# Seven half-size products for the last product of a graph layer, with PSUM copies and one buffer less, in a fused two-layer graph network on one Trainium2 core

## The chip, the core and the metric

The kernel runs on one core of a Trainium2 chip. The core has a matrix engine (PE, with its weight loads shown apart as PEld), a vector engine (DVE), a scalar engine (ACT), a general engine (POOL, not used here beyond the set-up) and a synchronising engine (SP) whose queue issues all DMA transfers. Each engine works through its own list of instructions in order, and waits at semaphores for the others. Data lies in HBM outside the core, in SBUF (128 partitions) for operands, and in PSUM for what PE writes. The metric is the device time of one execution in microseconds; the time of a version is the median of its runs.

## The reference

32 graphs ("batches") of 512 nodes with 512 features go through two layers, all in fp32. Layer 0 is attention with 8 heads of 64 whose weights are multiplied by the adjacency, an output product, a residual and a layer norm. Layer 1 is a graph attention with one logit per pair of nodes.

```python
# layer 0
q = x @ Wq.T + bq ; k = x @ Wk.T + bk ; v = x @ Wv.T + bv      # 8 heads of 64
logits = q k^T / sqrt(64) + log(clip(adj, 1e-8))
out = softmax(logits) v @ Wo.T + bo
x = layer_norm(x + out) * gamma + beta
# layer 1
feat_proj = feats @ fc_w.T + fc_b
q = feat_proj @ q_w.T + q_b ; k = feat_proj @ k_w.T + k_b       # one number per node
masked = q + k^T + (1 - adj) * -1e9 ; leaky ReLU, slope 0.01
out = softmax(masked) @ feat_proj + feats
```

## The kernel before

**Tiling.** A 512x512 matrix is held as four chunks of 128 partitions. N and D are 512, P is 128, H is 256 (half a row), KH is 2 (half the chunks). Layer 1 is computed as z = e^T-weighted sum of the normalised rows n (`z`, matmul group pz), and then zT times fc (`out_units`, group pg), so the projection by fc comes after the weighted sum. Each row of the result is scaled by 1/r and added to yb, the residual, and stored (L457, L460).

**Seven products.** Several 512x512 products are done as seven products of half-size blocks with sums of blocks ahead and behind (the scheme of Strassen in Winograd's form): q and k together (`seven_qk`, L587, banks called f), v (`seven_v`) and Wo (`seven_wo`), these two through `seven` (L199, groups pv and pw). Their PSUM banks have names a, b, c (and d). "First" in a call of `mul` tells whether the bank is started afresh or added to. Product 6 of Wo reads data that a subtraction on DVE has turned first (L718).

**Order.** The order on PE, DVE, ACT and SP is written out by hand (`manual_schedule`), so what a function calls first comes first in the engine's list. The main loop runs over batches b and, in each, over four slots p, one for each pair of heads (`slot`). A slot does the scores of its pair (`score`, tile sc, in the two double banks of the pool ps_s), exponentials on ACT (L772, into tiles `at`), the multiplication by adjacency on DVE (`factors`, L780), the sums for the denominator on DVE (`sums`, L790 and L793), the value product of the pair before (`values`, po), and q and k of the pair after (`seven_qk`, which takes both banks of ps_s in turn). Later stages of earlier batches are laid in between:

- slot 0: the transposed weights eT of batch b-2 (`eT`, four DVE transposes of the blocks eP), then z of b-2, then yb of b-2 (`rest_of_layer1`);
- slot 1: Wo of b-1, the statistics of the norm, and the mask of e (L396); x again into n, and adj into e of b-1, are loaded ahead of the slot (`load_again`);
- slot 2: norm rows of b-1 on ACT, xT of b+1 (four DVE transposes), the last product of layer 1 of b-2 (`out_units`), the dots with uk and uq of b-1 (`dots`, L370), the spreading of k by a trip through DRAM;
- slot 3: block differences for the next batch (`differences`, L568 to L571), v of b+1, q and k of its first pair, and the softmax of b-1 (`softmax`: `logits` L409 and L410, `weights` L420 and L421, then 16 DMAs that write e in blocks into eP).

In the last batch, slot 3 is `last_slot`, which ends with the whole of layer 1 for batches 30 and 31.

**Buffers.** The tag L1 has two buffers of 8 KB a partition, for e, eT and zT. The tag x of the pool io has one, for x, the work tile w, and eP. `at` has six buffers, `as` two, and the pool ps_m three banks.

Of the kernel before, what the change touches and what calls it, by code (L numbers as in the profile page):

```python
# [19 lines left out]
P = 128  # L20
# [5 lines left out]
BL = 32  # L26
# [4 lines left out]
def kernel(  # L31
# [48 lines left out]

    nc = tc.nc
# [8 lines left out]
    assert 2 * DK == P and N == 512 and D == 512 and B >= 2  # L90
# [46 lines left out]
    def spread_blocks(dst, src):  # L137


        for i in range(P // BL):  # L140
            for j in range(P // BL):
                nc.sync.dma_start(
                    out=dst[j * BL : (j + 1) * BL, i, :].rearrange("r (m f) -> r m f", f=BL),
                    in_=src[i * BL : (i + 1) * BL, :, :].rearrange(
                        "r c (t q f) -> q r (c t) f", q=P // BL, f=BL)[j],
                )
# [10 lines left out]
    def load_constants():  # L157
# [10 lines left out]
        for name in ("v_s", "wo_s"):  # L168
            K[name] = const.tile([P, 3, KH, H], FP, name=name)
# [35 lines left out]
    def fold_units(psum, scratch):  # L205
# [57 lines left out]
        def spread():  # L263
# [8 lines left out]
            ps = psum.tile([P, D], FP, tag="m", name="ps_parts")  # L272
# [163 lines left out]
    def z_units(s, psum, name):  # L436

        def unit(d):
            pz = psum.tile([P, N], FP, tag="m", name=f"pz_{name}_{d}")
            product(pz, lambda i: s["n"][:, i, ts(d, P)], lambda i: s["eT"][:, i, :])  # L440
            nc.scalar.copy(s["zT"][:, d, :], pz)  # L441
        return [lambda d=d: unit(d) for d in range(DC)]
# [24 lines left out]
    def fast(ctx):  # L467
# [31 lines left out]
        def load_again(b):  # L499
            s = S[b]  # L500
            if b == B - 1:
                s["n"] = act.tile([P, NC, D], FP, tag="xT", name=f"n_{b}")
            elif b > 0:
                s["n"] = act.tile([P, NC, D], FP, tag="n", name=f"n_{b}")
            if b > 0:
                load_b(s["n"], x[b])
            if b < B - 1:
                s["e"] = act.tile([P, NC, N], FP, tag="L1", name=f"e_{b}", bufs=2)
                load_b(s["e"], adj[b])

        def load_last_e():

            S[B - 1]["e"] = cT
            load_b(cT, adj[B - 1])
# [59 lines left out]
        def seven_qk(b, p):  # L574
# [18 lines left out]
            def one(name):  # L593
                if name == "b":
                    mul(2, ps["b"], True)
                    add.append(lambda: nc.vector.tensor_add(q[:, :H], ps["b"], q[:, :H]))  # L596
                elif name == "a":
                    mul(1, ps["a"], True)
                    nc.scalar.activation(q[:, :H], ps["a"], AF.Identity, bias=bq)  # L599
                elif name == "c":  # L600
                    mul(5, ps["c"], True)
                    nc.scalar.activation(k[:, H:], ps["c"], AF.Identity, bias=bk)
                elif name == "d":
                    mul(4, ps["d"], True)
                    nc.scalar.activation(k[:, :H], ps["d"], AF.Identity, bias=bk, scale=-1.0)
                elif name == "a6":
                    mul(6, ps["a"], False)
                    nc.scalar.activation(q[:, H:], ps["a"], AF.Identity, bias=bq)
                elif name == "c3":
                    mul(3, ps["c"], False)  # L610
                    add.append(lambda: nc.vector.tensor_add(q[:, H:], ps["c"], q[:, H:]))  # L611
                elif name == "a7":
                    mul(7, ps["a"], False)
                    add.append(lambda: nc.vector.tensor_add(k[:, H:], ps["a"], k[:, H:]))
                    add.append(lambda: nc.vector.tensor_add(k[:, :H], ps["a"], k[:, :H]))

            add = []
            own = p % 2 == 1

            def unit(names):  # L620
                if not ps:
                    f = [
                        ps_s.tile([P, 2, N], FP, tag="s", name=f"f_{b}_{p}_{i}") for i in range(2)
                    ]
                    for i, name in enumerate("acbd"):
                        ps[name] = f[i % 2][:, i // 2, :H]
                    if own:
                        ps["b"] = ps_m.tile([P, H], FP, tag="m", name=f"pq_{b}_{p}")
                add.clear()
                for name in names:  # L630
                    one(name)
                for a in add:
                    a()
# [3 lines left out]
            names = (("b", "a", "c"), ("a6", "d"), ("a7", "c3"))  # L637
            if not own:
                names = (("a", "c", "b", "d"), ("a6", "c3"), ("a7",))
            return [lambda n=n: unit(n) for n in names]  # L640

        def seven_v(b):
# [13 lines left out]
            def unit0():  # L656
# [3 lines left out]
                nc.scalar.copy(c11, ps["a"])  # L660
                mul(2, ps["b"], True)
                nc.vector.tensor_add(c11, ps["b"], c11)

            def unit1():
                mul(5, ps["c"], True)
                nc.scalar.copy(c22, ps["c"])
                mul(6, ps["a"], False)
                nc.scalar.copy(c12, ps["a"])

            def unit2():  # L670
                mul(4, ps["b"], True)
                nc.scalar.activation(c21, ps["b"], AF.Copy, scale=-1.0)
                mul(3, ps["c"], False)
# [8 lines left out]
        def seven_wo(b, banks, apart=False):  # L682
# [3 lines left out]

            s = S[b]
            n, oT = s["n"], s["oT"]
            put = b > 0
            n11, n12, n21, n22 = (  # L690
                n[:, m : m + KH, ts(h, H)] for m in (0, KH) for h in range(2)
            )
            wo, W = K["wo"], K["wo_s"]
            right = {1: wo[:, :KH, :H], 2: wo[:, KH:, :H], 3: wo[:, KH:, H:], 4: W[:, 2],
                     5: W[:, 0], 6: W[:, 1], 7: wo[:, :KH, H:]}
            ps = {}

            def data(i, c):
                return {1: oT[c][:, :H], 2: oT[KH + c][:, :H], 3: oT[KH + c][:, :H],
                        4: oT[KH + c][:, H:], 5: oT[c][:, H:], 6: oT[c][:, :H],  # L700
                        7: s["s3"][:, c, :]}[i]

            def mul(i, to, first):
                seven(data, right, i, to, first)

            def seed():
                for name, bank in zip("bac", banks()):
                    ps[name] = bank
                for name, h in (("a", 0), ("c", 1)):
                    bo = K["bo"][:, ts(h, H)].unsqueeze(1).to_broadcast([P, KH, H])  # L710
                    if put:
                        nc.scalar.copy(ps[name], bo)

            def unit0():
                mul(1, ps["a"], not put)
                mul(2, ps["b"], True)
                for c in range(KH):
                    nc.vector.tensor_sub(oT[c][:, :H], oT[c][:, H:], oT[c][:, :H])  # L718
                nc.vector.tensor_add(n11, ps["a"], n11)
                for c in range(KH):  # L720
                    nc.vector.tensor_sub(oT[KH + c][:, :H], oT[KH + c][:, :H], oT[c][:, :H])
                nc.vector.tensor_add(n11, ps["b"], n11)

            def unit1():
                mul(5, ps["c"], not put)
                mul(6, ps["a"], False)
                nc.vector.tensor_add(n22, ps["c"], n22)
                nc.vector.tensor_add(n12, ps["a"], n12)

            def unit2():  # L730
                mul(3, ps["c"], False)
                mul(7, ps["a"], False)
                nc.vector.tensor_add(n12, ps["c"], n12)
                nc.vector.tensor_add(n22, ps["a"], n22)

            def unit3():
                if apart:
                    mul(4, ps["b"], True)
                    nc.vector.tensor_add(n21, ps["a"], n21)
                    nc.vector.tensor_add(n21, ps["b"], n21)  # L740
                else:
                    mul(4, ps["a"], False)
                    nc.vector.tensor_add(n21, ps["a"], n21)
            return [seed, unit0, unit1, unit2, unit3]
# [6 lines left out]
        def other_banks(b):  # L751

            def tiles():
                return [t.rearrange("p (n f) -> p n f", n=KH) for t in (
                    ps_m.tile([P, N], FP, tag="m", name=f"pw_{b}_b"),
                    ps_o.tile([P, N], FP, tag="po", name=f"pw_{b}_a"),
                    ps_s.tile([P, 2, N], FP, tag="s", name=f"pw_{b}_c")[:, 0, :],
                )]
# [117 lines left out]
        def divide_here(b, p):  # L876
# [20 lines left out]
            def refine():  # L897
                junk = S[b - 1]["w"][:, 0, :]
# [9 lines left out]
        def z(b):  # L908
            s = S[b]
            s["zT"] = act.tile([P, DC, N], FP, tag="L1", name=f"zT_{b}", bufs=2)  # L910
            return z_units(s, ps_m, b)

        def eT(b):
            s = S[b]
            s["eT"] = act.tile([P, NC, N], FP, tag="L1", name=f"eT_{b}", bufs=2)
            if b >= B - 2:
                return transpose_units(s["e"], s["eT"], ps_m, nc.scalar.copy, f"e_{b}")

            eP = s["eP"].rearrange("p q (c t f) -> p t c q f", c=NC, f=BL)
            return [lambda t=t: nc.vector.transpose(  # L920
# [439 lines left out]
```

## Time and profile before

| what | value |
|---|---|
| median of 3 runs | 3525.23 us (3522.59 to 3525.47) |
| profiled execution | 3527.14 us, its span 3525.4 us |
| mean granted TensorE clock | 0.998 |
| DMA | 250.66 MB in the span, mean 71 GB/s |
| chain that ended last | PE 96%, DVE 2% |
| one batch in the middle (b=15) | 1505.76 to 1614.22 us |
| q, k, v, Wo: matmuls of 128x256 | mean 379 to 405 ns of one |
| scores, values, pz, pg: matmuls of 128x512 (or 64x512) | mean 592 to 617 ns of one |

How to read it: the page gives busy time, the mean duration of one instruction, and the idle time ahead of a group with what ended it. A group of matmuls has overlapping members, so its mean duration is longer than the distance from one start to the next. Every fp32 matmul of the program appears as two records. In a timeline, each line is a run of like instructions: start, length, engine, line, operation, output and inputs, how many, and in brackets how long the engine sat idle and for what. "DVE 2%" in the chain is the share of the span in which the last chain of work ran through DVE.

### The profile page before, as it was taken

What the parts mean: (1) busy time and instruction counts of PE and PEld (TensorE: products, weight loads), DVE (VectorE), ACT (ScalarE), POOL (GpSimd) and SP (SyncE); (2) the same over time, 40 slices, a digit from 0 to 9 for tenths busy, and PEclk for the clock granted to TensorE, in tenths of its full rate; (3) what the DMA queues carried; (4) which work ended last, traced back from release to release, by engine and by line L of the source; (5) the groups of instructions that cost most, each with busy time, mean ns of one, the idle gap of its engine ahead of it and who ended that gap; (6) DMA issues with size and microseconds to landing.
All of it is one profiled execution on the core that took longest, in us unless ns stands there. A gap on an engine that the chain in (4) does not pass through costs nothing.

```text
span 3525.4 us, 38493 instructions
## 1 busy us (share of the span) xinstructions
PE 3503.8 (99%) x13834; PEld 2041.8 (58%) x13834; DVE 2739.6 (78%) x4690; ACT 1305.6 (37%) x2120; POOL 0.9 (0%) x9
## 2 busy tenths in 40 slices
PE   9999999999999999999999999999999999999999
PEld 3555665655556656555566565555665655556654
DVE  5788778788787787777877878878778777787786
ACT  3334333433334343333433343333434333343332
POOL 0000000000000000000000000000000000000000
PEclk9999999999999999999999999999999999999999
DMA  4244233443233442334423344333344233442321
GB/s 114 49 75 88 51 70 70 73 87 58 71 73 62 87 75 58 75 61 81 88 52 70 70 73 88 58 71 73 62 87 77 56 76 61 81 88 53 69 64 52
DMA packets 880461, 250.66 MB, mean 71 GB/s; under 512 B 807180, under 2 KB 807436, under 8 KB 880264
## 3 DMA queue, kind: packets, MB, share of 16 engines
q1 hardware_dynamic: 880264, 248.15, 35.6%
q8 instruction: 110, 1.80, 0.2%
q14 instruction: 87, 0.71, 0.1%
HBM read 181.93 MB, written 34.65 MB: 61 GB/s over the span
## 4 chain that ended last, share of the span: by engine, by line
PE 96%; DVE 2%; issue 0%; DMA 0%; ACT 0%; SPq 0%; DVEq 0%; ACTq 0%
PE f L587 19%; PE sc L767 14%; PE po L805 13%; PE pg L304 12%; PE pz L304 12%; PE pw_a L199 6%; PE pv_a L199 5%; PE pw_c L199 3%; PE pv_b L199 3%; PE pv_c L199 3%; PE pq L587 2%; PE ps L822 2%; PE pw_b L199 2%; PE pk L304 0%; PE pv L304 0%; DVE at L780 0%
## 5 line engine op out<-in xcount | busy, mean ns | idle before, releaser
L772 ACT ACTIVATE at<-sc 128x1024 f32<-128x1024 f32 x512 | 496.5, 1021 | 788.3 <-PE sc L767 786.5
L780 DVE SCALAR_TENSOR_TENSOR at<-cT,at 128x1024 f32<-128x1024 f32 x512 | 601.7, 1217 | 175.2 <-ACT at L772 175.0
L767 PE MATMUL sc<-qT,kT 64*128 64x512 f32 x2048 | 510.6, 617 | 0.5 <-DVE qT L611 0.5
L805 PE MATMUL po<-at,v 128*64 128x512 f32 x2048 | 469.0, 600 | 0.0
L304 PE MATMUL pz<-eT,n 128*128 128x512 f32 x1024 | 445.4, 592 | 0.0
L304 PE MATMUL pg<-fc,zT 128*128 128x512 f32 (+1 forms) x1032 | 445.3, 589 | 0.0
L767 PEld LDWEIGHTS sc<-qT,kT 64*128 64x128 f32 x2048 | 176.7, 186 | 295.8 <-issue 268.2
L304 PEld LDWEIGHTS pg<-fc,zT 128*128 128x128 f32 x1032 | 195.8, 190 | 231.8 <-issue 215.2
L304 PEld LDWEIGHTS pz<-eT,n 128*128 128x128 f32 x1024 | 194.2, 190 | 231.0 <-issue 221.1
L805 PEld LDWEIGHTS po<-at,v 128*64 128x64 f32 x2048 | 135.7, 137 | 318.2 <-issue 315.3
L793 DVE TENSOR_TENSOR as<-as,at 128x1024 f32<-128x1024 f32 x254 | 308.3, 1214 | 5.5
L587 PE MATMUL f<-T,qk_s 128*128 128x256 f32 x992 | 244.8, 379 | 6.4 <-DVE qT L596 4.8
L441 ACT COPY zT<-pz 128x512 f32<-128x512 f32 x128 | 74.8, 585 | 425.4 <-PE pz L304 425.4
L587 PEld LDWEIGHTS f<-T,qk_s 128*128 128x128 f32 x992 | 185.0, 190 | 36.3 <-DVE qT L596 5.6
L587 PE MATMUL f<-xT,wq 128*128 128x256 f32 x744 | 191.0, 379 | 0.0
L813 ACT COPY oT<-po 128x512 f32<-128x512 f32 x128 | 75.1, 587 | 289.3 <-PE po L805 289.3
L790 DVE TENSOR_TENSOR as<-at,at 128x1024 f32<-128x1024 f32 x128 | 154.2, 1205 | 2.2
L587 PEld LDWEIGHTS f<-xT,wq 128*128 128x128 f32 x744 | 138.2, 190 | 22.4 <-ACT qT L599 0.2
L599 ACT ACTIVATE qT<-f,bq 128x256 f32<-128x256 f32 x124 | 58.7, 473 | 234.9 <-PE f L587 234.9
L587 PE MATMUL f<-xT,qk_s 128*128 128x256 f32 x496 | 128.0, 381 | 0.0
L587 PE MATMUL f<-T,wk 128*128 128x256 f32 x496 | 127.3, 379 | 0.0
L587 PE MATMUL f<-xT,wk 128*128 128x256 f32 x496 | 127.3, 379 | 0.0
(208 smaller groups left out, 4562.2 us busy)
## 6 DMA issues: line engine op xcount, KB each, us to landing
cT<-in_adj_dram SPq DMA_DIRECT2D x512, 64.0 KB
out_dram<-yb SPq DMA_DIRECT2D x127, 256.0 KB
R<-d SPq DMA_DIRECT2D x126, 256.0 KB
x<-in_x_dram SPq DMA_DIRECT2D x124, 256.0 KB
e<-in_adj_dram SPq DMA_DIRECT2D x31, 1024.0 KB
n<-in_x_dram SPq DMA_DIRECT2D x31, 1024.0 KB
eP<-e SPq DMA_DIRECT2D x480, 64.0 KB
w<-dk SPq DMA_DIRECT2D x32, 256.0 KB
```

Of the source, the lines that this page charges most:

```text
L199: nc.tensor.matmul(to[:, n, :], data(i, c)[:, ts(n, P)], weights[i][:, c, :], start=(first and n == 0 and c == 0), stop=(n == KH - 1 and c ...
L304: nc.tensor.matmul(ps, lhs(i), rhs(i), start=(i == 0), stop=(i == 3))
L441: nc.scalar.copy(s["zT"][:, d, :], pz)
L587: nc.tensor.matmul(to, left[i][:, c, ts(p, P)], s["B"][i][:, c, :], start=(first and c == 0), stop=(c == KH - 1), skip_group_check=True,)
L767: nc.tensor.matmul(sc[:, j, :], s["kT", p][rows, ts(kc, P)], s["qT", p][rows, :], start=True, stop=True,)
L772: nc.scalar.activation(at, sc, AF.Exp, scale=SCALE)
L780: nc.vector.scalar_tensor_tensor(at, cT[:, kc, :].unsqueeze(1).to_broadcast([P, 2, N]), ADJ_MIN, at, ALU.max, ALU.mult,)
L790: nc.vector.tensor_add(s["as", p], s["at", p, 0], s["at", p, 1])
L793: nc.vector.tensor_add(s["as", p], s["as", p], s["at", p, kc])
L805: nc.tensor.matmul(s["po", p][j * DK : (j + 1) * DK, :], s["v"][h // 4][:, kc, ts(h % 4, DK)], s["at", p, kc][:, j, :], start=(kc == 0), s ...
L813: nc.scalar.copy(s["oT"][p], s["po", p])
L822: nc.tensor.matmul(ps[h * BL : (h + 1) * BL, :], ones[:, :BL], s["as", p + h // 2][:, h % 2, :], start=True, stop=True,)
```

## The change

It has four parts, which go together.

- **The last product of layer 1** (`out_units`) is replaced, for batches 0 to 29, by seven products of half-size blocks (`seven_out`). It shares `seven_rows` with Wo. fc gets three sum blocks fc_s once (`combine_right`). The data blocks need two sums (`z_sums`, in slot 1) and two subtractions in slot 2. Products 1, 5, 2, 6, 3, 7 are in slot 2, product 4 in slot 3 (`rest`). The result is added to yb in 12 half-row operations, and stored in two DMAs of half a batch. The last two batches keep `out_units`; the one block of fc that was turned is turned back in `last_slot`.
- **The bank of the first product is copied inside PSUM**: product 1 is needed twice, and where it was read out and product 2 added by DVE, ACT now copies bank a to bank b, and product 2 is added to b by PE. This holds for q and k, v, Wo and the new product. q/k no longer starts with product 2 in a bank of ps_m. For batch 0 the banks of Wo are seeded with bo like the others, and `add_bo` is no longer called for it.
- **The tag L1 has one buffer**, for e and zT in turn. e of b-1 is therefore loaded in slot 3 of b (`load_e`), after the readers of zT, and masked in the same slot. n and x are loaded at the start of slot 1.
- **e is turned in place**: the 16 DMAs write the blocks so that four DVE transposes of eP in place give eT, and z reads eP through a view. Each of z's matmuls thus reads a part of all four transposed chunks.

Moves besides: the second half of the sums of pair 0 goes from slot 0 to slot 1, that of pair 2 from slot 2 to slot 3, and the first half of those of pair 3 to the end of slot 3; the reciprocals of the first two pairs (`divided`) go from slot 2 to slot 3.

```diff
-        for name in ("v_s", "wo_s"):
+        for name in ("v_s", "wo_s", "fc_s"):
...
-            product(pz, lambda i: s["n"][:, i, ts(d, P)], lambda i: s["eT"][:, i, :])
+            product(pz.rearrange("p (c n) -> p c n", c=NC), lambda i: s["n"][:, i, ts(d, P)],
+                    lambda i: s["eT"][:, i])
...
+            def unit0():
+                banks()
+                mul(1, ps["a"], True)
+                mul(5, ps["c"], True)
+                nc.scalar.copy(ps["b"], ps["a"])
+                nc.scalar.activation(k[:, H:], ps["c"], AF.Identity, bias=bk)
+
+            def unit1():
+                mul(6, ps["a"], False)
+                mul(2, ps["b"], False)
+                nc.scalar.activation(q[:, H:], ps["a"], AF.Identity, bias=bq)
+                nc.scalar.activation(q[:, :H], ps["b"], AF.Identity, bias=bq)
...
+        def seven_rows(data, sub, W, w, bank, add, apart=False):
...
+            def unit0(first):
+                mul(1, "a", first)
+                mul(5, "c", first)
+                nc.scalar.copy(bank("b"), bank("a"))
+
+            def unit1():
+                mul(2, "b")
+                mul(6, "a")
+
+            def unit2():
+                mul(3, "c")
+                mul(7, "a")
+
+            def unit3():
+                mul(4, "b" if apart else "a", apart)
+            end = [lambda: add(1, 0, "a")]
+            if apart:
+                end.append(lambda: add(1, 0, "b"))
+            return [unit0, unit1, unit2, unit3], [
+                [lambda: sub("11", "21", "11"), lambda: add(1, 1, "c")],
+                [lambda: sub("12", "12", "11"), lambda: add(0, 1, "a"), lambda: add(0, 0, "b")],
+                [lambda: add(0, 1, "c"), lambda: add(1, 1, "a")],
+                end,
+            ]
...
+        def seven_out(b):
...
+            def add(i, j, name):
                 for c in range(KH):
+                    row = i * KH + c
+                    o = yb[:, row, ts(j, H)]
+                    nc.vector.scalar_tensor_tensor(
+                        o, ps[name][:, c, :], r[:, row : row + 1], o, ALU.mult, ALU.add
+                    )
...
+            adds[2].insert(1, lambda: store(0))
+            adds[3].append(lambda: store(1))
+            return muls, adds
+
+        def z_sums(b):
...
+            nc.vector.tensor_sub(s["z3"], a11, a21)
+            nc.vector.tensor_add(a21, a21, a22)
...
-            s["zT"] = act.tile([P, DC, N], FP, tag="L1", name=f"zT_{b}", bufs=2)
+            s["zT"] = act.tile([P, DC, N], FP, tag="L1", name=f"zT_{b}")
...
-            eP = s["eP"].rearrange("p q (c t f) -> p t c q f", c=NC, f=BL)
-            return [lambda t=t: nc.vector.transpose(
-                s["eT"][:, t, :].rearrange("p (c q f) -> p c q f", c=NC, f=BL), eP[:, t]
-            ) for t in range(NC)]
+            s["eT"] = s["eP"].rearrange("p c (t n) -> p t c n", t=NC)
+            return transposes(s["eP"], s["eP"])
...
+            if p == 1 and last >= 0:
+                load_n(last)
+            if p == 1 and nxt < B:
+                load_x(nxt)
...
+            if p == 3:
+                run(rest[0] + rest[1])
+                if last >= 0:
+                    load_e(last)
...
+                if last >= 0:
+                    mask(S[last])
...
             if p == 1:
+                sums(b, 0, 1)
                 sums(b, p, 1)
...
+                    if b >= 2:
+                        z_sums(b - 2)
+                    for i in range(3):
+                        wos[i + 1]()
+                        run(wo_adds[i])
+                        next_qk[i]()
+                    next_qk[3]()
+                    wos[4]()
+                    run(wo_adds[3])
                     run(stats_units(S[last], small, last))
-                    mask(S[last])
...
                 vs[0]()
                 next_qk[0]()
-                units = softmax(last) if last >= 0 else []
                 run(units[:1])
+                sums(b, 2, 1)
+                if last >= 0:
+                    divided(b, 0)
...
                 turn_a((0, 1))
+                sums(b, p, 0)
                 sums(b, p, 1)
+
+        def layer1_rows(b, next_qk, norm):
...
+            muls, adds = seven_out(b - 2) if b >= 2 else ([], [[], [], [], []])
+            rest = ([], [])
+            for i in range(4):
+                next_qk[i]()
+                if i == 2:
+                    sums(b, 2, 0)
+                run(norm[i : i + 1])
+            run(muls[:1] + adds[0][:1])
+            if nxt < B:
+                run(xT(nxt))
...
+            ks, qs = dots(last)
+            run(adds[0][1:] + muls[1:2] + adds[1])
+            if nxt < B:
+                run(muls[2:3] + adds[2][:2] + ks[:1] + adds[2][2:] + ks[1:])
+                k_rows(last)
+                rest = (muls[3:], adds[3])
```

## The prediction

> **What bounds the kernel now.** I read the page's busy shares first, then the groups by form, then the timelines of PE, DVE, ACT and SP over one batch in the middle (b=15, 1505.76 to 1614.22 us), and last the stages of that batch for the DMA rate.
>
> ```profile
> PE 3503.8 (99%) x13834; PEld 2041.8 (58%) x13834; DVE 2739.6 (78%) x4690; ACT 1305.6 (37%) x2120; POOL 0.9 (0%) x9
> ...
> L304 PE MATMUL pg<-fc,zT 128*128 128x512 f32 x1016 | 441.8, 592 | 0.0
> ...
> 1543.40 1.89 PE L199 MATMUL pw_b<-wo,oT 128*128 128x256 f32 x8
> 1545.13 1.03 PE L587 MATMUL f<-xT,wq 128*128 128x256 f32 x4
> ...
> 1550.31 1.89 PE L199 MATMUL pw_a<-wo_s,oT 128*128 128x256 f32 x8
> ...
> 1574.65 13.90 PE L304 MATMUL pg<-fc,zT 128*128 128x512 f32 x32
> 1588.47 1.99 PE L767 MATMUL sc<-qT,kT 64*128 64x512 f32 x8
> ```
>
> PE has no holes: 99% busy, and of 3525.4 us only 21.6 are without a matmul. So time saved on PE counts in full, and so does every new wait of PE. Means of one matmul (592 ns) overlap with the next and are no price; starts are. From 1574.65 to 1588.47, 32 matmuls of 512 columns: 13.82 us, 432 ns each. From 1543.40 to 1545.13, 8 of 256 columns: 1.73 us, 216 ns. Half the columns cost half.
>
> ```profile
> 1518.26 2.48 DVE L920 STREAM_TRANSPOSE eT<-eP 128x512 f32<-128x512 f32 x4
> ...
> 1536.38 2.36 DVE L780 SCALAR_TENSOR_TENSOR at<-cT,at 128x1024 f32<-128x1024 f32 x2 [5.55 <-ACT at L772]
> 1538.78 1.23 DVE L790 TENSOR_TENSOR as<-at,at 128x1024 f32<-128x1024 f32 x1
> 1539.92 1.29 DVE L860 TENSOR_TENSOR oT<-oT,R 128x512 f32<-128x512 f32 x2
> 1541.13 0.75 DVE L874 TENSOR_TENSOR oT<-oT,oT 128x256 f32<-128x256 f32 x2
> 1541.89 2.36 DVE L780 SCALAR_TENSOR_TENSOR at<-cT,at 128x1024 f32<-128x1024 f32 x2
> 1544.17 2.47 DVE L793 TENSOR_TENSOR as<-as,at 128x1024 f32<-128x1024 f32 x2
> 1546.56 0.75 DVE L718 TENSOR_TENSOR oT<-oT 128x256 f32<-128x256 f32 x2
> ...
> 1564.00 1.19 DVE L396 TENSOR_SCALAR e<-e 128x2048 f32<-128x2048 f32 x1
> ...
> 1590.56 0.63 DVE L568 TENSOR_TENSOR T<-xT 128x512 f32<-128x512 f32 x1
> ```
>
> DVE is 78% busy, but it feeds PE at points with little room. L718 ends at 1547.2 and its reader, the sixth product of Wo, starts at 1550.31: 3.1 us of room. The four eT transposes end at 1520.66, and z starts at 1520.33, which is possible only because its first matmul needs the first transpose alone. The 5.55 us idle means that DVE's work in slot 1 is tied to PE: it starts 2.23 us after the slot's first score matmul (1534.15), however early DVE was.
>
> [...] The trace: n and e, 2.1 MB, are issued at 1534.25 and 1534.69 and move until about 1541.6 (stage rows of 0.5 us, 350 to 420 GB/s), 7.4 us[...]. [...] 605 ns for pw_a<-bo into PSUM against 585 for R<-ps out of it (128x512).
>
> **The change part by part.** Clocks below run from each slot's first score matmul: slots 0 to 3 at 1505.76, 1534.15, 1560.09, 1588.47, next batch 1614.22.
>
> Seven products. Per batch 32 x 432 ns = 13.82 us go; 7 x 8 x 216 ns = 12.08 come: -1.74 us. Batches 0 to 29 use it (30 and 31 keep the old form): 30 x 1.74 = -52 us. PSUM copies: in wo, v and out they lie behind the product that PE does next (copy 0.6 us, next product 1.73): nothing. In q/k, the first product ends 0.16 us after its last start, the copy takes 0.47 (row L599, 128x256), done 0.63 us after PE went on, and the next product lasts 0.86: nothing; were the copy 0.8, 0.1 us each.
>
> Slot 0, banks. Before, product b went first, into its own bank, while ACT was reading both score banks. Now the first product needs the third exponential finished: it starts at 1513.44 and lasts 1.02, ends 1514.46, against PE ready at 1514.28. The second needs the fourth (1515.38). With the hand-over +0.35 us, 31 times: +11 us (0.1 to 0.6 each). In slot 2 the ps matmuls (1.0 us) lie in between: nothing.
>
> Slot 0, e. The in-place blocks make the first z matmul need all four transposes. DVE, from v's add at 1505.87 (held by PE) to the transposes, gets the first half of sums for pair 3 ahead (L790, 1.18): last transpose done at 1520.66 + 1.18 = 1521.84, +0.05. PE is ready at 1520.33 + 0.35 = 1520.68. Wait 1.2 us, take 1.15 (0.5 to 2.2, more if the blocks' DMAs come later); 30 times: +35 us.
>
> Slot 1. DVE starts at 1536.38 as before and reaches 1544.17 + 2.40 = 1546.56 after its two sums. Ahead of the first subtraction now come two more sums of pair 0 (2.40) and two z sums (L569's kind, 0.65 each, 1.3): it ends at 1547.24 + 3.7 = 1550.9, clock 16.8. PE wants it earlier: products 1 and 5 (1.83, 1.73), two of q/k (0.86 each), 2 (1.73) from 1541.57 put product 6 at 1548.6, clock 14.4. Wait 2.4 us, 30 times, and 1.1 in batch 1, which has no z sums: +73 us (1.9 to 2.9 each). Behind product 6 in PE's queue stand the rest of q/k, Wo, and slot 2; nothing gives it back, since slot 2's DVE work is tied to PE again. DVE sheds the mask here (L396, 1.1 us), after the point of the wait.
>
> Slot 2. PE ends 3.46 us earlier (12.08 less product 4, moved to slot 3: clock 24.9 instead of 28.4). DVE's last k add ends at clock 16.1. Then: subtraction 0.65 after product 1 (17.2), four xT transposes 2.40 (19.6), add c 0.78, subtraction 0.65 (21.0), adds of a and b after product 6 (23.2), of c after 3 (24.2), one dot 0.75, add of a after 7 (25.9), seven dots and small ones 5.6: 31.5. (An add is two of L457's 128x256, 0.39 apart, estimated from 484 ns less the overlap of its neighbours.) PE's products find their operands ready: no wait. But DVE enters slot 3 at clock 6.6; before, 1590.56 was clock 2.1.
>
> Slot 3. Differences 2.59 (9.2), last add 0.78 (10.0), two factors 2.3 (12.3), then the mask, which needs e. Before, e came two slots ahead; now SP issues the store of yb, which waits for that last add, then e: 10.0. Store 0.5 MB and e 1 MB against 2.1 MB in 7.4 us: 0.5 MB less at 390 GB/s is 1.3, so 6.1 us: e at 16.2. DVE idles 3.9 us. Then mask 1.1 (17.4), factors 2.3 (19.7), logits 2.84 and 0.36 (22.9), sums of pair 2 2.36 and reciprocal 0.6 (25.9), weights 2.4 (28.3), of which ACT's exponentials end 1.1 later (29.4), then ACT's v and k (0.5 each, 30.3), then DVE's last k add: 30.8. The next batch's scores need that k. PE would be ready at 25.75 + 1.73 = 27.5: wait 3.3 us (2.1 if e need not queue behind the store's bytes, 5 if cT loads crowd it), 29 times (batches 2 to 30): +96 us. Had e been there, DVE would end at 26.9: hidden.
>
> Head and tail: four more DVE operations once, the last slot with some 2 us more DVE work: 0 taken (-3 to +5). Sum: -52 + 11 + 35 + 73 + 96 = +163. The profiled execution took 3527.1 us (span 3525.4): 3690. The median of the runs is 1.9 us below it: 3688.
>
> **The rivals.** (1) The mechanism above, period 108.46 + 5.4: 3688. (2) e comes in time, because DVE reaches the store's add by clock 7 or so: the slots 0 and 1 waits remain, 163 - 96 = +67: 3592. For it: DVE is idle 23 us a batch (108.46 - 2739.6/32), which might shift; against: its start in slot 3 follows from PE's product 7. (3) Other side: the waits of a batch come to less than the 1.74 us gained. The point that decides is the first subtraction of slot 1: DVE's list between clocks 2.23 and 16.8 would have to end by 14.4. If it does, DVE is ahead of PE everywhere and only the banks' wait is left: -52 + 11, 3486. Against: every duration in that list is a row of this trace, and the list is worked off in order. (4) Worse: the blocks' DMAs start after the late exponentials (16 issues, 10.8 us at 1503.91) and pass the DVE's transposes: 2 to 3 us more a batch, 3765. (5) Half products not at half price (379 ns each): 56 x 379 = 21.2 us, +7.4 a batch; the starts speak against it.
>
> **How the numbers follow.** (1) 68%, (2) 17%, (3) 8%, (4) 6%, (5) 1%. The range 3585 to 3740 holds (1) with its bounds (slots 0 and 1: 0.9 lower or 1.8 higher a batch, slot 3: 2.1 to 5, not all at once), and (2); (3) and most of (4) stay out. Within 0.2% is +-7 us, about what a measurement of this kernel can tell from no change; only a narrow strip between (3) and (2) falls there: 2%. Faster 7%, slower 91%.
>
> **What would show it.** Right: PE holes ahead of Wo's product 6 (on DVE's subtraction, 2.4 us), ahead of z (on the eP transposes, 1.2), and at the batch's first scores (on the k add); mask waiting for the DMA of e; the out products 12.1 us a batch. Wrong: no hole at product 6, or a mask that never waits; a strided z operand (pz) slower than 432 ns a start; copies into PSUM over 0.8 us.

## The result and the profile after

| | before | after |
|---|---|---|
| median of runs | 3524.61 us (3522.59 to 3525.47) | 3777.97 us (3772.19 to 3780.09) |
| profiled execution, its span | 3527.14, 3525.4 us | 3779.30, 3777.5 us |
| mean granted TensorE clock | 0.998 | 0.982 |
| one batch in the middle | 108.46 us | 116.57 us |

After takes 1.0717 times as long as before (95% interval 1.0699 to 1.0736): 253 us more. The prediction had 163 more. Its direction and three of its four holes are there. What slot 3 loses, product 4 apart, is nearly twice as much as predicted (5.83 us for 3.3), it is lost at another place, and with a consequence that the prediction did not price.

The page of after first: busy shares, the chain that ended last, then two of the costly groups (busy time and mean ns of one, then the idle time ahead of the group and what ended it).

```profile
PE 3564.9 (94%) x14554; PEld 2233.8 (59%) x14554; DVE 2788.9 (74%) x4865; ACT 1384.9 (37%) x2339; POOL 0.9 (0%) x9
...
PE 46%; DVE 32%; DMA 8%; issue 5%; SPq 5%; ACT 4%; DVEq 0%; ACTq 0%
...
L205 PE MATMUL pv_b<-wv,T 128*128 128x256 f32 x248 | 100.2, 575 | 102.4 <-ACT v L659 102.4
L205 PE MATMUL pw_a<-wo_s,oT 128*128 128x256 f32 x504 | 126.6, 395 | 62.6 <-DVE oT L732 62.6
```

The same columns in the groups by form: first, of after, the product of v that comes next behind the one that waits; then, of before, these two products:

```profile
L205 PE MATMUL pv_c<-v_s,xT 128*128 128x256 f32 x248 | 68.6, 426 | 0.0
```

```profile
L199 PE MATMUL pv_b<-wv,T 128*128 128x256 f32 x248 | 59.6, 384 | 0.0
...
L199 PE MATMUL pv_c<-v_s,xT 128*128 128x256 f32 x248 | 58.6, 379 | 0.0
```

PE is no longer in nearly the whole of the chain that ends last (96% before, 46% now). Most of PE's waiting is ahead of three groups: a product of v, 102.4 us in all; product 6 of Wo, 62.6; and z, 12.0. The second thing to see is in the column of means: the product of v took 384 ns a record before and takes 575 now, and the next takes 426 for 379, with the same operands and count. They are not only late, they are slow: 40.6 and 10.0 us more for the same work, 51 us beside the 102.4 of waiting.

Now one batch, slot by slot, from the starts of the first score matmuls (after: 1598.18, 1628.40, 1656.42, 1681.44, next batch 1714.75):

| slot | before | after | difference | predicted |
|---|---|---|---|---|
| 0 | 28.39 | 30.22 | +1.83 | +1.5 |
| 1 | 25.94 | 28.02 | +2.08 | +2.4 |
| 2 | 28.38 | 25.02 | -3.36 | -3.46 |
| 3 | 25.75 | 33.31 | +7.56 | +5.03 (product 4, 1.73, and the wait, 3.3) |
| batch | 108.46 | 116.57 | +8.11 | +5.47 |

2.53 of the 2.64 us that a batch is over the prediction lie in slot 3. Here are PE's three longest holes in that batch, with the product behind the last (start, length, engine, line, operation, operands, count; in brackets the idle time ahead and what ended it):

```profile
1614.47 14.00 PE L310 MATMUL pz<-eP,n 128*128 128x512 f32 x32 [0.40 <-DVE eP L527]
...
1645.00 1.99 PE L205 MATMUL pw_a<-wo_s,oT 128*128 128x256 f32 x8 [2.01 <-DVE oT L732]
...
1705.36 3.42 PE L205 MATMUL pv_b<-wv,T 128*128 128x256 f32 x8 [3.94 <-ACT v L659]
1708.61 1.89 PE L205 MATMUL pv_c<-v_s,xT 128*128 128x256 f32 x8
```

And what DVE, ACT and SP do ahead of the long hole, one fence for each:

```profile
1699.36 1.23 DVE L402 TENSOR_SCALAR e<-e 128x2048 f32<-128x2048 f32 x1 [5.60 <-DMA e<-in_adj_dram]
```

```profile
1703.50 1.33 ACT L415 ACTIVATE w<-w,q 128x512 f32<-128x512 f32 x2 [5.54 <-DVE top L416]
1704.74 0.56 ACT L659 COPY v<-pv_b 128x512 f32<-128x512 f32 x1
```

```profile
1691.52 0.41 SPq L764 DMA_DIRECT2D out_dram<-yb  x1
1692.02 0.41 SPq L129 DMA_DIRECT2D e<-in_adj_dram  x1
1692.65 13.13 SPq L500 DMA_DIRECT2D cT<-in_adj_dram  x16
```

Read from the bottom: the store of yb is issued at 1691.52, clock 10.1 of the slot (predicted 10.0), and e behind it. The mask can start at 1699.36, clock 17.9 (predicted 16.2). DVE stands for 5.60 us. In ACT's list the third and fourth logit stand behind DVE's logits, which stand behind the mask; and the copy that empties v's bank b stands behind those two in ACT's list. PE's next product into bank b waits for it. So e's lateness reaches PE through two in-order lists at v's product, some 9 us ahead of the k add where the prediction looked for it. The k add itself is hardly earlier than PE, though:

```profile
1714.01 0.41 DVE L631 TENSOR_TENSOR kT<-f,kT 128x256 f32<-128x256 f32 x1
```

It ends at 1714.42, and the next batch's scores, which need it, start at 1714.75. DVE and ACT come to it through the softmax, which e has held up as well. So even without the hole at v this batch could have been only some 0.2 us shorter.

The last view is of PE in stretches of 1 us across the end of the hole: stretch, its length, busy time with number of matmuls, granted clock, DMA share, GB/s.

```profile
1704.00:1705.00 1.00, 0.00 (x0) 0.93 0.81 128
1705.00:1706.00 1.00, 0.64 (x2) 0.50 0.78 122
1706.00:1707.00 1.00, 1.00 (x4) 0.50 0.81 127
1707.00:1708.00 1.00, 1.00 (x4) 0.50 0.00 0
1708.00:1709.00 1.00, 1.00 (x5) 0.86 0.00 0
```

The granted clock goes to 0.50 near the end of the hole and stays there for 3.4 us (from 1704.86 in the record of the clock). A product that takes 1.73 us from start to start takes 3.25 there (1705.36 to 1708.61).

### The profile page after: what moved, and what is told of

Its sections match the earlier page's. It is cut to its first block, busy times and chain, and to the rows that moved or that the text cites. A ratio compares the mean times of both kernels' runs of the same rounds, so it can differ in the third digit from the quotient of the medians.

```text
span 3777.5 us, 40530 instructions
## 1 busy us (share of the span) xinstructions
PE 3564.9 (94%) x14554; PEld 2233.8 (59%) x14554; DVE 2788.9 (74%) x4865; ACT 1384.9 (37%) x2339; POOL 0.9 (0%) x9
## 4 chain that ended last, share of the span: by engine, by line
PE 46%; DVE 32%; DMA 8%; issue 5%; SPq 5%; ACT 4%; DVEq 0%; ACTq 0%
PE pz L310 12%; PE f L596 9%; DVE at L820 7%; DVE as L833 6%; DMA e<-in_adj_dram 5%; PE pw_a L205 5%; PE sc L807 5%; PE pw_o_a L205 4%; SPq L147 4%; DVE w L376 4%; PE po L845 3%; PE pw_o_c L205 3%; ACT e L427 2%; DVE eP L527 2%; DVE oT L900 1%
## 5 line engine op out<-in xcount | busy, mean ns | idle before, releaser
L310 PE MATMUL pz<-eP,n 128*128 128x512 f32 x960 | 420.0, 595 | 12.0 <-DVE eP L527 12.0
L310 PEld LDWEIGHTS pz<-eP,n 128*128 128x128 f32 x960 | 179.9, 190 | 239.3 <-issue 215.3
L596 PE MATMUL f<-xT,wq 128*128 128x256 f32 x992 | 262.6, 387 | 8.3 <-ACT at L812 8.3
L596 PE MATMUL f<-T,qk_s 128*128 128x256 f32 x992 | 250.7, 386 | 0.0
L596 PEld LDWEIGHTS f<-xT,wq 128*128 128x128 f32 x992 | 185.2, 191 | 83.3 <-ACT at L812 60.0
L626 DVE TENSOR_TENSOR qT<-f,qT 128x256 f32<-128x256 f32 x124 | 52.3, 421 | 226.7 <-ACT kT L625 226.7
L205 PE MATMUL pv_b<-wv,T 128*128 128x256 f32 x248 | 100.2, 575 | 102.4 <-ACT v L659 102.4
L205 PE MATMUL pw_a<-wo_s,oT 128*128 128x256 f32 x504 | 126.6, 395 | 62.6 <-DVE oT L732 62.6
L619 ACT ACTIVATE qT<-f,bq 128x256 f32<-128x256 f32 x124 | 59.2, 477 | 283.9 <-PE f L596 283.9
L402 DVE TENSOR_SCALAR e<-e 128x2048 f32<-128x2048 f32 x30 | 36.8, 1227 | 149.1 <-DMA e<-in_adj_dram 149.1
L205 PEld LDWEIGHTS pw_a<-wo_s,oT 128*128 128x128 f32 x504 | 94.9, 193 | 87.2 <-DVE oT L732 75.0
```

The source lines that it names most:

```text
L205: nc.tensor.matmul(to[:, n, :], data(i, c)[:, ts(n, P)], weights[i][:, c, :], start=(first and n == 0 and c == 0), stop=(n == KH - 1 and c ...
L310: nc.tensor.matmul(ps, lhs(i), rhs(i), start=(i == 0), stop=(i == 3))
L596: nc.tensor.matmul(to, left[i][:, c, ts(p, P)], s["B"][i][:, c, :], start=(first and c == 0), stop=(c == KH - 1), skip_group_check=True,)
```

## The experiments

All are edits of the changed kernel. Each time is the median, with the ratio to before and its 95% interval; "gain" is against after's 3778. Theory A, from the trace of after: e is late, and the length of the batch follows from it through v's bank b, with the half clock on top; the other waits are those predicted. Rivals: e's lateness is hidden by something else that ends as late (the k add, or DVE's list), or the transfer itself can't be faster.

**1. e issued ahead of the adds and the second store** (slot 3):

```diff
-                run(rest[0] + rest[1])
+                run(rest[0])
                 if last >= 0:
                     load_e(last)
+                run(rest[1])
```

> The changed kernel with one swap in slot 3: SP issues the load of e as soon as product 4 has read zT, ahead of the store of yb (the add of product 4 still comes where it was). Theory (e is late because SP holds it behind a store that waits for DVE): e is issued about 6.5 us earlier, the mask no longer waits (5.6 us before), ACT's second pair of logits no longer holds the copy that frees bank pv_b, PE's hole of 4.1 us and the half clock after it (1.5 us) go: 5.6 us in 29 batches, 163 us, about 3615. Rival 1 (DVE has too much work in slot 3 anyway, e only shows it): the wait moves to the k add ahead of the next batch's scores, at most half is gained, 3700 or more. Rival 2 (e is crowded by cT's small packets and lands late however it is issued): the mask still waits 2 us or more, some 3700.

3660.61 us, ratio 1.0382 (1.0364 to 1.0399), a gain of 117. The clock is at 0.991. So e's lateness is the largest cause, but the gain is less than the 163 expected. PE in slot 3 of this run:

```profile
1655.83 2.00 PE L205 MATMUL pv_b<-wv,T 128*128 128x256 f32 x8 [0.69 <-ACT v L659]
...
1665.04 1.99 PE L807 MATMUL sc<-qT,kT 64*128 64x512 f32 x8 [1.17 <-DVE kT L631]
```

The mask still waits 2.35 us (to 1649.83; 38.5 us in all, 149.1 in after). In this batch both places stop PE, a little each; over the run, v's bank does so in 9 batches alone (5.4 us in all), and the k add in 30 (27.6 us, 4.4 in after). Of the 46 us that are missing, the k add's wait is thus 23, and 15 more are slow clock, which now comes behind the hole at product 6 (its group is busy for 142.1 us, 126.6 in after; more on these holes in the last section). SP's list shows why e is late once more:

```profile
1641.03 0.34 SPq L395 DMA_DIRECT2D w<-dk  x1
1641.41 0.43 SPq L129 DMA_DIRECT2D e<-in_adj_dram  x1
```

e was put ahead of the store, but it is behind the trip of k through DRAM, which holds SP to 1641.37. It is issued at clock 6.2, and the mask starts 8.4 us later.

**2. PE kept busy in the hole.** Four matmuls of 512 columns (8 records, some 3.4 us), whose result nothing uses, ahead of the product that waits:

```diff
                 run(units[1:])
+                if b >= 2:
+                    fill = ps_o.tile([P, N], FP, tag="po", name=f"fill_{b}")
+                    product(fill, lambda i: K["wv"][:, i, :P], lambda i: K["wo"][:, i, :])
                 vs[2]()
```

> The changed kernel with four extra 512-column products (8 records, 3.5 us of PE) into the idle bank po, put in PE's list just where it waits for bank pv_b in slot 3; their result is not used. Theory (the hole of 4.1 us makes the granted clock fall to half, and the pv_b product that follows takes 3.25 us where it takes 1.73): the hole is filled, the clock stays, and although there is more work each batch from 2 to 30 is 1.5 us shorter: 3735. Rival (the long pv_b product comes from something else, such as ACT working on its bank): no gain, 3778 or longer.

3762.51 us, ratio 1.0670 (1.0653 to 1.0688), a gain of 15.5, where 43 was expected. The half clock after this hole is gone from the batch shown: in the timeline the product takes its 1.73 us again, on the same operands (1700.65 to 1702.38). But the next limit stands right behind:

```profile
1700.65 1.89 PE L205 MATMUL pv_b<-wv,T 128*128 128x256 f32 x8
...
1709.74 1.99 PE L807 MATMUL sc<-qT,kT 64*128 64x512 f32 x8 [1.16 <-DVE kT L631]
```

In all, by the waits of this run, the next batch's scores stand 35.0 us for DVE's last k add, which in after they did for 4.4. This is the wait that the prediction named. In after the half clock behind the hole took up nearly all of it. In sum, the two products of v give back 48 us (121.1 us busy in this run for 168.8 in after), the scores take 31 of it, and 12 go at product 6, whose group has grown from 126.6 to 138.5 us (the last section has more on it). The ps matmuls of the pairs' denominators give 9 (81.0 us for 90.3), and the added matmuls take about what the wait at v's bank took before. That makes 14 of the 15.5.

**3. Wo's subtraction ahead of the moved sums** (slot 1): the second half of pair 0's sums and the two z sums are taken behind the adds of Wo's second step, instead of ahead of the subtraction.

```diff
                 sums(b, p, 1)
-                sums(b, 0, 1)
...
-                    if b >= 2:
-                        z_sums(b - 2)
                     for i in range(3):
                         wos[i + 1]()
                         run(wo_adds[i])
+                        if i == 1:
+                            sums(b, 0, 1)
+                            if b >= 2:
+                                z_sums(b - 2)
```

> The changed kernel with two sums of pair 0 and the two z sums moved on DVE, in slot 1, from ahead of Wo's first subtraction to behind the adds of product 6 and 2. Theory (the wait of product 6 comes from these 3.7 us ahead of its subtraction): the hole of 2.2 us at product 6 goes and DVE's gaps between Wo's later adds take the work in: 30 x 2.2 = 66 us, 3712. Rival (DVE is short of time in slot 1 as a whole): the wait comes back at product 4, which needs bank a read out, or at the next slot's norm: gain under 20 us.

3697.66 us, ratio 1.0494 (1.0472 to 1.0517), a gain of 80. The hole at product 6 is gone altogether (62.6 us in the waits of after, no row in this run's). The prediction had put it at 73. In the timeline product 6 takes 1.89 us (at 1607.61 and at 1722.60), its time at full clock.

**4. First half of pair 3's sums ahead of the mask** (slot 3; DVE then does them while it waits for e, and not at the head of slot 0):

```diff
             if p == 3:
                 load_a(nxt, (0, 1))
+                sums(b, p, 0)
...
                 turn_a((0, 1))
-                sums(b, p, 0)
                 sums(b, p, 1)
```

> The changed kernel with the first half of the sums of pair 3 (1.2 us of DVE) moved from the end of slot 3 to ahead of the mask, where DVE waits for e. Theory (slot 0's waits, 0.8 us at ps and 0.6 us at z, come from DVE's list being 1.2 us too long): both shrink, 1.2 us in 30 batches, 36 us, 3742. Rival (z waits for the DMAs that bring the blocks of e): only the wait at ps goes and z waits as long as before: gain under 10 us.

3744.66 us, ratio 1.0620 (1.0602 to 1.0638), a gain of 33. Slot 0 of this run:

```profile
1717.92 14.00 PE L310 MATMUL pz<-eP,n 128*128 128x512 f32 x32
```

No wait is left at z, and the ps matmuls (the denominators of pair 3) take 1.06 us in place of 1.84. In after they stood 0.8 us for the last of these sums, a wait which the prediction had missed: it followed DVE's list to the transposes, and not to the readers of the sums on the way.

**5. e still earlier**: product 4 is taken in slot 2, so that the buffer comes free before slot 3, and e is loaded there.

```diff
-                if last >= 0:
-                    load_e(last)
...
-                run(muls[2:3] + adds[2][:2] + ks[:1] + adds[2][2:] + ks[1:])
+                run(muls[2:3] + adds[2][:2] + ks[:1] + adds[2][2:] + muls[3:])
+                load_e(last)
+                run(ks[1:])
                 k_rows(last)
-                rest = (muls[3:], adds[3])
+                rest = ([], adds[3])
```

> The changed kernel with product 4 of the last product put at the end of slot 2 instead of into slot 3 (the same PE work, one place earlier), and the load of e issued right behind it, ahead of the small transfers that spread k and of the second store. e_first showed e still issued behind the spreading of k, 6.2 us into slot 3, and a mask that waited 2.35 us. Theory (slot 3's loss is the late arrival of e and nothing else): e lands before DVE comes to the mask; the waits that e_first had left (0.69 us for bank pv_b and 1.17 us for the k add) go: 29 x 1.9 = 54 us below e_first, about 3607. Rival (DVE's own list in slot 3 is too long): the k add still holds the scores by a microsecond a batch, 3635 or more.

3660.42 us, ratio 1.0384 (1.0368 to 1.0400): the gain of experiment 1 and no more, where about 3607 us was expected. The mask no longer waits at all, v's bank hardly (0.1 us), and the scores wait for the k add in 2 batches alone (3.2 us), so the way from e is clear; but product 4 itself, straight behind product 7 in slot 2, now waits for DVE to empty bank a (30.8 us in this run's waits). One hole was traded for another that costs the same.

**6. The same, with DVE's sums of pair 2 moved out of slot 3 as well**, into its idle time in slot 2.

> e_early with all three sums of pair 2 (3.6 us of DVE) moved into the 4.3 us in which DVE waits in slot 2. If e alone was the cause in slot 3, the time is that of e_early within 10 us, since DVE then only waits longer elsewhere. If DVE's list was part of it, it is 25 us or more below e_early.

3659.43 us, ratio 1.0382 (1.0366 to 1.0397): no difference from experiment 5. With e there in time and product 4 in slot 2, the length of DVE's list in slot 3 does not matter. That rival falls for this version.

**7. All moves together**: 3, 4 and 6, and in slot 0 the divisor of pair 2 (`divide`) behind the factors. The expectation names a move of the ps matmuls in slot 0 as well; the kernel that ran does not have it.

> e_early_s2 with the moves of wo_first (two sums and the z sums behind Wo's sixth product) and of sums3 (a sum of pair 3 ahead of the mask), and with the ps matmuls of slot 0 put between the scores and q/k, as slot 2 has them, so that they cover the wait for the banks. Theory (the seven products are worth 1.74 us a batch, and the waits account for everything else): all new waits gone, 3525 - 52 = 3473, with 10 us left over for small ones up to 3485. Rival (something that no wait shows, such as z's operand read in pieces, costs time too): above 3500.

3530.35 us, ratio 1.0015 (1.0009 to 1.0022), at 98% busy PE and clock 0.998. That is a gain of 248, but some 50 less than expected, and still not under before. It is above the 3500 that the expectation gave for its rival, a cost that no wait shows. But waits account for most of it. What is left in the waits (who waited for whom, us in all, times, longest):

```profile
PE pw_o_a L205 <- DVE yb L759: 32.4, 30, 4.3
```

That is product 4's bank, from experiment 5; z waits 9.0 more. Experiment 8 takes these two away.

**8. Product 4 back in slot 3, e first on SP.** From 7: product 4 returns to the place where its bank has been free for long; e follows it at once; dk and w, which stood ahead of e in experiment 1, come behind it; and slot 0's `first_difference` goes behind the transposes of eP. The lines for product 4 and SP, against after:

```diff
-                run(rest[0] + rest[1])
+                run(rest[0])
+                if last >= 0:
+                    load_e(last)
+                    k_rows(last)
+                run(rest[1])
```

> All four moves again, but the fourth product of out goes back to slot 3, behind the first half of the scores, where its bank has been free since long before; e's load follows it at once and the dk and w transfers stand behind e on SP. Slot 0's first difference is taken behind the transposes of eP. If the 1.13 us before product 4 and the 0.3 to 0.4 us before z are what keeps all_moves at before's time, 29 x 1.13 + 30 x 0.35 = 43 us go: 3487, 1.1% under before. Rival: e, issued at clock 4 to 5 instead of in slot 2, is late for the mask again by about 1 us and the hole comes back at v's product 4 or at the next scores, as in e_first (0.69 and 1.17 us): 3530 to 3545.

3484.25 us, ratio 0.9884 (0.9868 to 0.9901): 1.2% under before, and within 3 us of what was expected. It is the only version that beats both. Its busy shares:

```profile
PE 3455.5 (99%) x14554; PEld 2198.6 (63%) x14554; DVE 2794.5 (80%) x4865; ACT 1390.3 (40%) x2339; POOL 0.9 (0%) x9
```

PE is in 94% of the chain that ends last, and between 1592.71 and 1699.53, the same matmul in two batches, it has no hole: a period of 106.82 us, 1.64 under before's 108.46. That is what the seven products were said to be worth, 1.74, but for 0.1. No cost is left that no wait shows: the matmuls of z, with the operand in pieces, have a mean of 592 ns here (417.1 us, x960), as before. How much each of the three edits of this step brings was not taken apart.

**9. The first half of the adjacency loads later in the program**, to see whether these transfers of 64 KB crowd e:

```diff
-                load_a(nxt, (0, 1))
...
-                load_a(nxt, (2, 3))
+                load_a(nxt, (0, 1, 2, 3))
```

> The changed kernel with one edit: the first half of the next adjacency's 16 small transfers no longer follows e on SP but goes with the second half, later in the slot. If those small packets crowd e, e lands 1.5 to 1.7 us earlier than at clock 17.9, the mask waits about 4 us instead of 5.6, the hole at v's product 4 shrinks by as much to about 2.3 us, and the half clock after it mostly goes too: 29 x 1.6 to 29 x 3.1, 3690 to 3730. Rival: e's own transfer takes the time however little is beside it: mask wait unchanged within 0.3 us, 3770 to 3780.

3772.38 us, ratio 1.0702 (1.0684 to 1.0720). This tells nothing of the theory, because the edit did not move the transfers:

```profile
1690.18 0.41 SPq L129 DMA_DIRECT2D e<-in_adj_dram  x1
1690.81 12.79 SPq L500 DMA_DIRECT2D cT<-in_adj_dram  x16
```

All 16 are issued 0.63 us behind e (1690.18 to 1690.81), as in after (1692.02 to 1692.65), though their call stands later in the program: they were still next in SP's own list, and nothing between the two places made it wait.

The question can be read from two other runs instead. In stretches of 1 us from e's issue (stretch, length, SP's busy time, DMA share, GB/s), first the run of experiment 8, where SP issues e at 1668.39 and the next transfer, dk, only at 1673.63; then after:

```profile
1669.40:1670.40 1.00, 1.00 0.66 150
1670.40:1671.40 1.00, 1.00 0.96 291
1671.40:1672.40 1.00, 1.00 1.06 412
1672.40:1673.40 1.00, 1.00 0.51 197
```

```profile
1694.00:1695.00 1.00, 1.00 0.87 143
...
1696.00:1697.00 1.00, 1.00 1.06 412
...
1698.00:1699.00 1.00, 1.00 1.34 154
```

Alone, e's bytes (150 + 291 + 412 + 197 is 1,050 KB, the whole of it) are through by about 1673.0 (in half microseconds, 348 GB/s up to 1672.90 and 45 in the next), 4.6 us behind the issue at 1668.39. These 4.6 us end with the last bytes. In after it is 7.3 us from issue to mask (1692.02 to 1699.36), and there are stretches in which the DMA engines are as busy as in the others (shares of 0.87 and 1.34) while the rate falls to 143 and 154 GB/s. So, as an estimate from these two runs, up to 2.7 us of e's way in after come from its company, the store of yb ahead and the transfers of cT behind; the step from the last byte to the mask's start, which the run of experiment 8 does not show because its mask does not wait, is in these 2.7 too. How they share it was not settled.

## Why the prediction was right or wrong

**The seven products: right.** Product follows product at 1.73 us (1670.99 to 1672.71 in after), so 12.1 us a batch as predicted, and experiment 8 shows 1.64 of the 1.74 us as time, once nothing waits. Rival 5, half products not at half price, is out.

**PSUM copies: right, at nothing.** In after the copy of 128x256 takes 0.36 us, of 128x512 0.57, below the 0.47 and 0.6 assumed, and no product waits for one.

**Slot 0, banks: right.** 0.27 us of wait, and 0.33 from ready to start (1607.37 to 1607.70), for 0.35; 8.3 us in all for 11.

**Slot 0, z: mechanism right, split wrong.** z waits for the transposes as predicted, but for 0.40 us and 0.57 from ready to start, not 1.15. The difference went to a wait 11 us earlier that was not in the list, the ps matmuls for the same moved sum (1.84 us in place of about 1.0). Together 1.34 for 1.15. Experiment 4 removes both with one move, which shows the sum as their common cause.

**Slot 1: right.** 2.01 us of wait for 2.4, on the subtraction named, 62.6 us in all for 73. Experiment 3 shows the cause, the four sums put ahead of it.

**Slot 2: right.** 25.02 us for 24.92, and the store at clock 10.1 for 10.0. The list of DVE's operations, row by row through slots 2 and 3 to that store, was off by 0.1 us.

**Slot 3: mechanism right, size wrong, and this is the step that failed.** The prediction had "wait 3.3 us (2.1 if e need not queue behind the store's bytes, 5 if cT loads crowd it)", 29 times, +96 us. Slot 3 took 5.83 us more, product 4 apart, 2.53 over the 3.3. Two terms on the prediction's own path were too small:

- *e's landing*, which is most of it. "so 6.1 us: e at 16.2". It was 7.8, at 17.9. This makes 1.7 us. The cT loads behind e had been put into the range alone, though the trace of before has their 16 issues in the same slot. That these loads make the difference, and not the store ahead, is not shown: experiment 9 did not move them.
- *From the mask to the k add.* The prediction had 14.6 us from the mask's start to the end of the last k add (16.2 to 30.8). It is 15.06 in after (1699.36 to 1714.42), and within 0.01 us the same in experiments 1 and 2: 0.5 us more. So on this path the k add ends at clock 33.0, and these two terms are 2.2 of the 2.53 us.

Two things were missing:

- *Where the wait falls.* "The next batch's scores need that k" was true, but v's bank b needs ACT's copy first, and that stands behind the logits in ACT's list. The chain was followed along DVE to the end of the slot, and ACT's list was entered only there. The hole in the batch shown is 3.94 us (102.4 us in all, so 3.4 on average). Experiment 2 shows the k add as the second limit, near enough to take over at once: 15.5 us was all that the run gained.
- *What a long hole does to the clock.* Not in the prediction at all. After the hole of 3.94 us the next products run at 0.50: 1.5 us in the batch shown, 51 us in all from the two groups' busy times. In after 28 of the 30 holes at v's product (2.9 to 4.7 us) have a half clock at their end or behind them. A predicted wait of 3.3 us, with a bound of 5, was priced without it.

So v's hole and the slow clock are where PE's time went, but they are not what made the batch longer than predicted: with e as late as it was, the k add would have held PE nearly as long.

In sum over the run, as PE spent it, from the groups and waits of after: -52 for the products, 102.4 and 51 for v's hole and the clock behind it, 62.6 for product 6, 24 for the ps matmuls (31 x 0.77), 12.0 for z, 8.3 for the banks and 4.4 for the scores: +213 of the 252 us by which the spans differ. The starts of z, product 6 and v's product are later by another 0.16 to 0.18 us than these waits count (from the start of the product ahead and its time from start to start: 0.57 us for a wait of 0.40 at z, 4.12 for 3.94 at v's product), some 15 more, and slow clock behind product 6's hole 10 (its group and that of the q and k product behind it are busy for 126.6 and 250.7 us, 122.3 and 244.8 before). The last 14 were not traced.

The range's upper end lay 52 us above the forecast. Slot 3's excess alone, 2.53 us in 30 batches, is 76.

## What to carry to other kernels

Follow a late transfer along every in-order list that it stops, not only that of the engine that waits for it. Here PE stopped first at a bank whose reader was queued behind the stopped work, and a second limit ended almost at the same time: taking away the first gave 15 us of the 153 that were lost there. A predicted hole of PE needs a term for the clock as well: here a half clock came with 28 of 30 holes of 2.9 to 4.7 us (1.5 us in the batch shown) and with 6 of 31 holes of 2.0 to 2.2. And a change that pays on PE alone (1.6 us a batch here) is lost to any list order that makes PE wait: the same products cost 253 us or brought 41, and the whole difference lay in the places of a few pieces of DVE work and of the transfers of e and k on SP.

## What the hardware showed besides

Shorter holes than v's were followed by a half clock too. In after it came with the hole at product 6 (2.01 us in 30 batches, 2.22 in one) in 6 of 31 batches. In experiments 1 and 2, with 62.6 and 62.7 us of wait there in all as in after (62.6), this product's group is busy for 142.1 and 138.5 us, 126.6 in after.

The trace's record of the granted clock shows when. In after it has 38 stretches at 0.50: 35 of 3.41 us, two of 6.83 and one of 2.80 at the end. They start whole multiples of 3.413 us apart, to within 0.01 us. The four of before (at 14.79, 127.43, 195.69 and 3523.69) do so too. Here is PE in steps of this length across the hole at product 6, first in experiment 2, then in after, where the steps are counted from the starts of its half clocks (stretch, length, PE's busy time with number of matmuls, clock, DMA share, GB/s):

```profile
1636.16:1639.57 3.41, 1.39 (x7) 1.00 0.00 0
1639.57:1642.98 3.41, 3.41 (x9) 0.50 0.00 0
```

```profile
1640.01:1643.42 3.41, 2.98 (x14) 1.00 0.39 46
1643.42:1646.84 3.42, 1.84 (x9) 1.00 0.00 0
1646.84:1650.25 3.41, 3.41 (x17) 1.00 0.01 2
```

The holes are alike. In experiment 2 the idle time falls into one step, PE is busy for 41% of it, and the next step is slow. In after it falls across two steps, of which PE is busy for 87% and 54%, and no slow step follows. In the whole trace of after, cut into such steps, PE was busy for 42% or less of the step ahead of each of the 38 changes to half clock, and for 44% or more of each of the 1,028 full-clock steps behind which the clock stayed full. In before it was 49% or less ahead of its 4 changes, and 51% or more of each of 1,023 others. (A first step that holds the start of the program is left out in both.) Ends of matmuls are modelled in a trace, so these shares are estimates. What sets the clock was not shown.

A copy from PSUM to PSUM on ACT took 0.36 us for 128x256, less than the activation of 128x256 from PSUM to SBUF beside it (0.47 to 0.48, L614 and L619). Whether the operation or the target makes this difference was not taken apart; at 128x512 a copy took as long into PSUM (0.57, L653) as into SBUF (0.56, L659).
